# Moving the feed-forward's transposes from TensorE to 32 by 32 squares on VectorE and an exchange through DRAM

## The chip, the cores and the metric

The kernel runs on one core of a Trainium2 chip. The metric is the device time of one execution in microseconds (us); the time before is a median of three runs, 879.62 us (879.28 to 879.94). The engines are named as the profile names them: PE is TensorE (PEld its weight loads), DVE is VectorE, ACT is ScalarE, POOL is GpSimd, and SP issues the transfers ("SPq" is its queue). All are in-order; between engines an instruction waits for semaphores.

## The reference

Three layers work on x, 16 batches of 64 tokens with 512 features, each added to its input: cross-attention from a context of 512 tokens per batch, a differential self-attention, and a feed-forward whose operands are quantised to FP4 and back. Only the last concerns the change:

```python
def fp4_quant_dequant(x):                       # blocks of 16 along the last dim
    xb = x.reshape(shape[:-1] + (shape[-1] // BLOCK, BLOCK))
    scale = jnp.max(jnp.abs(xb), axis=-1, keepdims=True) / 6.0
    scale = jnp.maximum(scale, jnp.float32(1e-12))
    xn = xb / scale
    idx = jnp.searchsorted(_MID, jnp.abs(xn))
    q = _GRID[idx] * jnp.sign(xn) * scale

def fp4_linear(x, w):
    return jnp.einsum('bsk,nk->bsn', fp4_quant_dequant(x), fp4_quant_dequant(w))

x = x + fp4_linear(silu(fp4_linear(xn, w_gate)) * fp4_linear(xn, w_up), w_down)   # xn = layernorm(x)
```

The hidden width is 1408. Both activations, the normalised x and the hidden h, are quantised with the features along the free dimension, tokens on the partitions; the products want the features on the partitions. So both have to be transposed between the quantisation and the product that reads them.

## The kernel before

**Tiles and steps.** The 1024 tokens are eight tiles of 128. The hidden width is cut into three chunks of 512, 512 and 384 (`CHUNKS`). A step of the feed-forward is one (tile, chunk) pair; `FeedForward.steps` lists all 24: (0,0), (0,1), (1,0), (1,1), (0,2), (1,2), then (2,0), (2,1), (2,2) and so on to (7,2). The first three are spread by hand over the end of the self-attention, in `SelfAttention.rest`; `FeedForward.rest` calls `step(n)` for the others.

**One step.** Products run in three terms, high times high, high times low, low times high, over four 128-deep pieces: `terms`, L121, 12 matmuls for a chunk of 512. `gate` and `up` give 24 such matmuls into a PSUM pair. `gated` applies Silu on ACT (L1759) and the product with up on DVE (L1760). `quantise` calls `fp4_steps`: DVE's block maximum (L194), two small steps that make the scale and its shaded copy (L195, L196), the reciprocal (L197), the scaling by it (L199), a mask that keeps the exponent bits (L202), a Relu on ACT that turns them into a rounding constant (L205, called "the exponents' step" here), two scalar_tensor_tensor steps that round (L207, L208) and the scaling back (L210). All of h's DVE-capable steps are on DVE; for x both scalings are on POOL. `turn_h` for the step two back transposes h in 128 by 128 pieces on PE against an identity (L171) into PSUM, and `split` (L129, L130) makes the upper half by a rounding cast on ACT and the lower half by a subtraction on DVE. `down` for the step three back multiplies the halves with the down weights; after the third chunk the output tile is added up (L1812) and stored (L1813).

**x.** `norm(t+2)` is called in step (t,2): moments, the normalised tile, and the same quantisation with POOL's scalings. `turn(t+1)` transposes it on PE in step (t,1) and splits it.

**Order.** The scheduler orders each engine's instructions by a timing estimate of its own. At the end of `SelfAttention.rest`, `in_order` fixes the order of every engine's instructions as they are written up to there, by a dependence of each on the one before. What `FeedForward.rest` adds is free: the scheduler may put it between and in front of the fixed ones, and does. The last written lines of the fixed part are the upper half and product for (0,0)'s turn, the output product of tile 7 (`out(NT-1)`, the matmuls named wo) and the loads of the last weights; the loads of the third chunk's up-weights go into the slots that hold Wo until then.

**Buffers.** Gate and up alternate between two PSUM pairs. The halves of h have two buffers each (`two_h`, `two_l`). The exponents' tile `qe` is a single buffer (tag "one") that x and h share.

## Time and profile before

| | before |
|---|---|
| median of three runs | 879.62 us |
| the profiled execution's own time | 881.33 us |
| its span in the profile | 879.5 us |
| granted TensorE clock | 1.00 |
| matmuls for transposes of h (128x128) | 88, from 694.4 to 872.9 us |
| matmuls for transposes of x in the feed-forward | 32, from 665.7 to 836.1 us |
| output stores in the feed-forward, 256 KB each | 7, and 2 of 128 KB for the last tile |

The busy times on the page count the time in which an engine executes; matmuls are pipelined and their ends are modelled, so the start of one to the start of the next is the better measure of what an instruction costs PE. On the timeline a line is a group of like instructions: start, length, engine, line, operation, tiles, shapes, count, and in brackets the idle time before it and who ended it. The feed-forward's free part begins at about 694 us; from about 739 us on it repeats every 24.3 us, one token tile.

### The profile page before, as it was taken

To read this page: it belongs to the slowest core of one execution; us is meant where nothing else is said; L and a number is where in the kernel's file an instruction comes from. 1 tells how busy PE (TensorE), PEld (TensorE's weight loads), DVE (VectorE), ACT (ScalarE), POOL (GpSimd) and SP (SyncE) were. 2 spreads that over 40 slices of the span, in tenths; PEclk is the share of its full clock that TensorE was granted. 3 is DMA by queue.
4 is the path that set the end of the run, shared out by engine and by line. 5 is a ranking of instruction groups with operands and counts; after the bars stand their busy time and mean duration, and the time that the engine had idled before them with its cause. 6 is when DMAs were issued, how large, how long until landed. Compare 5 with 4: busy or idle time off the path is not lost.

```text
span 879.5 us, 17521 instructions
## 1 busy us (share of the span) xinstructions
PE 871.7 (99%) x6743; PEld 719.2 (82%) x6743; DVE 687.2 (78%) x1457; ACT 398.8 (45%) x787; POOL 296.2 (34%) x341
## 2 busy tenths in 40 slices
PE   8999999999999999999999999999999999999998
PEld 8988787878787888778878888888888888888887
DVE  7734457789788887787888867688998897888876
ACT  5654454544544535354445455554556233332221
POOL 2334234235353352353433622545543120111100
PEclk9999999999999999999999999999999999999999
DMA  8464554644655455435644362240008330000000
GB/s 277 167 233 169 167 163 142 201 143 141 192 164 160 138 174 168 136 111 178 183 134 149 121 198 64 82 192 1 1 3 320 136 144 13 13 13 13 13 12 25
DMA packets 80379, 111.12 MB, mean 126 GB/s; under 512 B 33176, under 2 KB 39080, under 8 KB 79016
## 3 DMA queue, kind: packets, MB, share of 16 engines
q1 hardware_dynamic: 80136, 109.48, 38.2%
q8 instruction: 53, 0.87, 0.4%
q0 software_dynamic: 160, 0.52, 0.2%
q14 instruction: 30, 0.25, 0.1%
HBM read 84.26 MB, written 25.72 MB: 125 GB/s over the span
## 4 chain that ended last, share of the span: by engine, by line
PE 93%; DVE 3%; DMA 2%; ACT 1%; POOL 1%; issue 1%; SPq 0%; ACTq 0%; DVEq 0%; POOLq 0%
PE pv L121 20%; PE pk L121 19%; PE gu L121 13%; PE dn L121 6%; PE sim L967 4%; PE av L1055 4%; PE Wv L121 3%; PE wo L121 3%; PE po L121 2%; PE Wq L121 2%; PE Wk L121 2%; PE prt L1004 2%; PE lq L121 2%; PE lk L121 2%; PE lv L121 1%; PE ht L171 1%
## 5 line engine op out<-in xcount | busy, mean ns | idle before, releaser
L121 PE MATMUL pv<-xvh,x 128*128 128x512 f32 x512 | 133.0, 394 | 0.0
L121 PE MATMUL pk<-x,xkh 128*128 128x512 f32 x512 | 128.2, 392 | 0.0
L121 PEld LDWEIGHTS pv<-xvh,x 128*128 128x128 f32 x512 | 94.8, 188 | 26.2 <-issue 7.0
L121 PEld LDWEIGHTS pk<-x,xkh 128*128 128x128 f32 x512 | 94.9, 188 | 19.5 <-issue 0.4
L990 ACT ACTIVATE pr<-pr,least 128x576 f32<-128x576 f32 x64 | 49.1, 769 | 59.7 <-DVE least L986 59.7
L941 DVE TENSOR_TENSOR k<-pk,row 128x512 f32<-128x512 f32 x64 | 43.2, 675 | 39.2 <-PE pk L121 39.0
L368 POOL TENSOR_TENSOR x<-raw,x 128x512 fp32r<-128x512 f32 x32 | 41.6, 1301 | 85.8 <-ACT x L362 80.5
L121 PE MATMUL pv<-xvl,x 128*128 128x512 f32 x256 | 68.7, 390 | 0.0
L121 PE MATMUL pk<-x,xkl 128*128 128x512 f32 x256 | 68.5, 389 | 0.0
L954 ACT ACTIVATE v<-pv,rs 128x512 f32<-128x512 f32 x64 | 43.2, 684 | 54.8 <-PE pv L121 54.3
L121 PE MATMUL gu<-uT,fx 128*128 128x512 f32 (+1 forms) x288 | 67.0, 377 | 0.2 <-DMA uT<-u_d 0.2
L121 PE MATMUL gu<-gT,fx 128*128 128x512 f32 (+1 forms) x288 | 65.8, 376 | 0.0
L121 PEld LDWEIGHTS gu<-gT,fx 128*128 128x128 f32 x288 | 52.2, 188 | 7.6 <-ACT fx L129 0.2
L121 PEld LDWEIGHTS gu<-uT,fx 128*128 128x128 f32 x288 | 51.8, 188 | 7.7 <-DMA uT<-u_d 0.5
L121 PEld LDWEIGHTS pv<-xvl,x 128*128 128x128 f32 x256 | 48.0, 188 | 10.3
L121 PEld LDWEIGHTS pk<-x,xkl 128*128 128x128 f32 x256 | 48.1, 188 | 10.2
L986 DVE CUSTOM_DVE_ANT_0 pr<-sim,mask 128x576 f32<-128x576 f32 x64 | 45.8, 753 | 5.3 <-PE sim L967 4.3
L205 ACT ACTIVATE qe_h<-qe_h,mmagic 128x512 f32<-128x512 f32 (+1 forms) x24 | 16.5, 687 | 66.7 <-DVE qe_h L202 64.6
L321 DVE BATCH_NORM_STATS2 cst<-nat 128x6 f32<-128x512 f32 x64 | 42.8, 669 | 3.7 <-DMA nat<-in_ctx_dram 3.7
L121 PE MATMUL dn<-dT,hh 128*128 128x512 f32 x170 | 42.9, 392 | 0.0
L967 PE MATMUL sim<-k,mask 64*64 64x288 f32 x512 | 40.4, 415 | 0.3 <-DMA mask<-q_d 0.3
L362 ACT CAST x<-raw 128x512 fp32r<-128x512 f32 x64 | 39.1, 631 | 0.0
(347 smaller groups left out, 1867.1 us busy)
## 6 DMA issues: line engine op xcount, KB each, us to landing
nat<-in_ctx_dram SPq DMA_DIRECT2D x16, 1024.0 KB
raw<-in_ctxT_dram SPq DMA_DIRECT2D x64, 256.0 KB
d_d<-qhl_d SPq DMA_DIRECT2D x11, 512.0 KB
row<-rs_d SPq DMA_DIRECT2D x16, 256.0 KB
g_d<-qhl_g SPq DMA_DIRECT2D x8, 512.0 KB
u_d<-qhl_u SPq DMA_DIRECT2D x8, 512.0 KB
gT<-g_d SPq DMA_DIRECT2D x4, 1024.0 KB
uT<-u_d SPq DMA_DIRECT2D x4, 1024.0 KB
```

The source lines that it names most:

```text
L121: self.nc.tensor.matmul(ps, lhsT=p[i], rhs=p[j], start=start and n == 0, stop=stop and n == last)
L205: nc.scalar.activation(e, e, AF.Relu, bias=self.mmagic, scale=MAGIC)
L321: nc.vector.bn_stats(st, self.nat[b][:, j, :])
L362: self.cm.nc.scalar.copy(self.done[b][0][:, c, :], self.raw[:, c, :])
L368: by.tensor_tensor(lo, self.raw[:, c, :], f32(hi), ALU.subtract)
L941: nc.vector.tensor_tensor(k[:, S : S + N], ps, cx.row[b], ALU.mult)
L954: nc.scalar.mul(v, ps, cx.rs[b][:, t : t + 1])
L967: nc.tensor.matmul(pss[r][c * S : (c + 1) * S, h, :half], lhsT=queries[b % 2][rows, m, :], rhs=st["k"][m][rows, at : at + half], start=Tru ...
L986: nc.vector.tensor_tensor_reduce(two(pr), ps[:, :, :half], two(mask), -1.0, BIG, ALU.add, ALU.min, least)
L990: nc.scalar.activation(pr, pr, AF.Exp, bias=least, scale=-1.0, accum_out=st["tot"][:, t : t + 1])
L1004: nc.tensor.transpose(pt[:, c, at : at + S], state[b]["pr", a][rows, r, first + j * P : first + (j + 1) * P], cm.ident[rows, rows],)
L1055: nc.tensor.matmul(st["av"][r][rows, a, :], lhsT=prT[:, j, rows], rhs=st["v"][j][:, at : at + S], start=False, stop=j == NJ - 1, skip_grou ...
```

## The change

The transposes of x for tiles 3 to 7 and of h for 19 of the 24 steps (`far_steps`, all but the first three and the last two) leave PE. DVE transposes each 32 by 32 square in place within its block (`squares`), SP stores the result to DRAM in four pieces of 32 partitions, and loads it back with squares exchanged, into a tile with features on the partitions. `halves` makes the upper half with a copy on ACT and the lower half with a subtraction on POOL, both from SBUF. The copy is ordered behind the last written exponents' step (`behind`). In a step with a far turn, `turn_h` is written behind the quantisation and the sending of the current step; in the two steps past the end it is written behind `down`. The last scaling of a far h moves to POOL. Two small steps of every quantisation become scalar_tensor_tensor with a constant tile as second tensor. At the end of `FeedForward.rest`, PE's order is fixed as written, from the first instruction on.

```diff
+        self.least = const.tile([P, D // BLK], F32, tag="least", name="least")
+        nc.gpsimd.memset(self.least, 1e-12)
+        self.none = const.tile([P, D // BLK], F32, tag="none", name="none")
+        nc.gpsimd.memset(self.none, 0.0)
...
-    def in_order(self):
+    def in_order(self, *only):
 
         last = {}
         for ins in self.nc.cur_bb.bb.instructions:
+            if only and ins.engine not in only:
+                continue
...
-        nc.vector.tensor_scalar(s, m, 1.0 / 6.0, 1e-12, ALU.mult, ALU.max)
-        nc.vector.tensor_scalar(m, s, 1.0 + SHADE, None, ALU.mult)
+        least, none = (t[:, :nb] for t in (self.least, self.none))
+        nc.vector.scalar_tensor_tensor(s, m, 1.0 / 6.0, least, ALU.mult, ALU.max)
+        nc.vector.scalar_tensor_tensor(m, s, 1.0 + SHADE, none, ALU.mult, ALU.max)
...
+        self.sq = [dram(f"sq_d{n}", [4, 32, 4, KC * 32]) for n in range(4)]
...
+        self.far, self.far_steps = 0, self.steps[3:-2]
...
+    def newest(self):
+        return self.nc.cur_bb.bb.instructions[-1]
+
+    def behind(self, ins):
+        self.tc.add_manual_dep(
+            ins,
+            self.exponents.name,
+            mybir.DependencyInfo(mybir.DependencyClass.NoSync, mybir.DependencyReason.DATA),
+            reason="behind",
+        )
+
+    def squares(self, src, nk, pool, tag, home, name):
+        nc = self.nc
+        t = self.w1.tile([P, 4, KC * 32], F32, tag=tag, name=f"sq_{name}")[:, :, : nk * 32]
+        nc.vector.transpose(
+            t.rearrange("p q (k l) -> p q k l", l=32),
+            src.rearrange("p (k q l) -> p k q l", q=4, l=32),
+        )
+        far = self.sc.sq[self.far % len(self.sc.sq)][:, :, :, : nk * 32]
+        self.far += 1
+        for n in range(4):
+            nc.sync.dma_start(far[:, :, n].rearrange("q f r -> f q r"), t[n * 32 : (n + 1) * 32])
+        raw = pool.tile([P, 4, KC * 32], F32, tag=home, name=f"sr_{name}")[:, :, : nk * 32]
+        nc.sync.dma_start(raw, far.rearrange("q f t r -> (q f) t r"))
+        return raw
+
+    def halves(self, hi, lo, raw):
+        src = raw.rearrange("p t (k l) -> p k t l", l=32)
+        hi, lo = (x.rearrange("p k (t l) -> p k t l", l=32) for x in (hi, lo))
+        self.nc.scalar.copy(hi, src)
+        self.behind(self.newest())
+        self.nc.gpsimd.tensor_tensor(lo, src, f32(hi), ALU.subtract)
+
+    def send(self, t):
+        self.st["zs", t] = self.squares(self.st.pop(("z", t)), KC, self.w2, "k1", "four0", f"x_{t}")
+
+    def send_h(self, n):
+        s = self.steps[n]
+        if s in self.far_steps:
+            pool, home = ((self.w1, "k2"), (self.w2, "sq"))[n % 2]
+            nk = CHUNKS[s[1]][1] // P
+            self.st["hs", s] = self.squares(self.st.pop(("h", s)), nk, pool, "k0", home, f"h_{s[0]}_{s[1]}")
+
+    def regroup(self, t):
+        both = self.w2.tile([P, 2, KC, P], F32R, tag=f"fx{t % 2}", name=f"fx_{t}")
+        self.halves(both[:, 0], both[:, 1], self.st.pop(("zs", t)))
+        self.st["x", t] = both[:, 0], both[:, 1]
...
     def quantise(self, s):
         t, c = s
-        self.cm.fp4(self.w2, self.st["h", s], CHUNKS[c][1], f"h_{t}_{c}", tag="one")
+        w = self.st["h", s]
+        steps = self.cm.fp4_steps(
+            self.w2, w, CHUNKS[c][1], f"h_{t}_{c}", False, s in self.far_steps, tag="one"
+        )
+        for n, _ in enumerate(steps):
+            if n == 2:
+                self.exponents = self.newest()
...
     def turn_h(self, s):
...
+        self.st["hT", s] = hh, hl
+        if s in self.far_steps:
+            self.halves(hh, hl, self.st.pop(("hs", s)))
+            return
         pt = cm.tr(f"ht_{t}_{c}")
         cm.transpose_chunks(pt, self.st.pop(("h", s)), nk)
...
     def step(self, n):
         s = self.steps[n] if n < len(self.steps) else None
         if s:
             self.gate(s)
-        if 0 <= n - 2 < len(self.steps):
+        near = s and self.steps[n - 2] not in self.far_steps
+        if near:
             self.turn_h(self.steps[n - 2])
         if s:
             self.up(s)
             self.hidden(s)
+            self.send_h(n)
+        if s and not near:
+            self.turn_h(self.steps[n - 2])
+        if s:
             if s[1] == 2 and 2 <= s[0] < NT - 2:
                 self.norm(s[0] + 2)
+                self.send(s[0] + 2)
             elif s in ((1, 1), (0, 2)):
                 self.norm(1 + s[1])
+                if s[1] == 2:
+                    self.send(1 + s[1])
         if 0 <= n - 3:
             self.down(self.steps[n - 3])
+        if not s and n - 2 < len(self.steps):
+            self.turn_h(self.steps[n - 2])
         if s and (s == (1, 2) or (s[1] == 1 and 2 <= s[0] < NT - 1)):
-            self.turn(s[0] + 1)
+            if s[0] == 1:
+                self.turn(s[0] + 1)
+            else:
+                self.regroup(s[0] + 1)
 
     def rest(self):
         for n in range(3, len(self.steps) + 3):
             self.step(n)
+        self.cm.in_order(mybir.EngineType.PE)
```

## The prediction

> **What bounds the kernel now.** I read the page's busy table first, then TensorE's timeline through the feed-forward, then ACT, DVE and POOL over the same stretches, then the busy time of each engine by stage.
>
> ```profile
> span 879.5 us, 17521 instructions
> PE 871.7 (99%) x6743; PEld 719.2 (82%) x6743; DVE 687.2 (78%) x1457; ACT 398.8 (45%) x787; POOL 296.2 (34%) x341
> 763.20:787.60 24.40, 24.40 (x124) 20.95 (x122) 21.57 (x47) 7.22 (x12) 2.21 (x2) 1.00 0.03 12
> ```
>
> TensorE bounds it. The third line is one token tile of the feed-forward (columns: window, length, then PE, PEld, DVE, ACT, POOL busy, clock, DMA share, GB/s): PE has no gap, DVE is busy 21.57 of 24.4 us, POOL 2.21. So work taken off PE counts in full, and every new wait of PE counts in full too. Only two PE gaps of any size stand after 694 us: 0.18 for the last up-weights and 0.41 at the very end.
>
> **What is removed.** By start-to-start times of the PE timeline four transposes take 0.36 us of the engine (694.51 to 694.87), three take 0.245 (854.37 to 854.62). Moved off are twelve 4-chunk and seven 3-chunk blocks of h, and x for tiles 3 to 7: 17 x 0.36 + 7 x 0.245 = 7.84 us. The 0.18 wait goes too (below): 8.0 us gained. The Trainium skill speaks against such a move: "VectorE: DVE Perf Modes", Rules for kernel authors, gives a 128x128 transpose to TensorE where PSUM will do, and its section on the three paths prices one on TensorE at 390 ns (bf16). By that figure 89 of them would save an estimated 34.7 us; the trace's 0.09 us apiece decides.
>
> **What TensorE's fixed order costs at the start.** Before, the scheduler slid the feed-forward's gate and up in front of the last output product; in the order written that product (wo of tile 7) comes straight after the ht transposes of chunk (0,0).
>
> ```profile
> 694.51 0.60 PE L171 MATMUL ht<-ident,h 128*128 128x128 f32 x4
> 694.87 2.98 PE L121 MATMUL gu<-gT,fx 128*128 128x512 f32 x12
> 697.68 2.88 PE L121 MATMUL gu<-uT,fx 128*128 128x512 f32 x12
> 700.40 1.07 PE L121 MATMUL wo<-Woh,oh 128*128 128x512 f32 x4
> ...
> 695.84 0.72 ACT L205 ACTIVATE qe_h<-qe_h,mmagic 128x512 f32<-128x512 f32 x1 [3.69 <-DVE qe_h L202]
> 696.46 0.76 ACT L1529 ACTIVATE oT<-ot,lnwb 128x512 f32<-128x512 f32 x1
> 697.26 0.62 ACT L1539 CAST oh<-oT 128x512 fp32r<-128x512 f32 x1
> ```
>
> wo needs oh, which ACT ends at 697.88, behind a relu that waits on DVE. ACT's order there is already fixed and is not touched. PE stands from 694.87 to about 698.0: 3.1 us. wo then ends at 700.7, not 703.6; the last up-weights reuse Wo's slots, so their load starts 2.9 us sooner and lands near 708.5, before it is wanted at 711: the 0.18 is gone. Next, turn(2) now stands right before gate (2,0). From the start of an xt to the first matmul that reads its cast is 1.37 us (723.41 to 724.78 in the trace, then covered by four down matmuls): 1.37 - 0.36 = 1.0 us open.
>
> **What the hold costs at the end.** The upper half of chunk (7,0) now stands on ACT behind the exponents of (7,2), whose chain starts when up (7,2) ends at 864.80. Before, that cast was done during up (7,2).
>
> ```profile
> 864.80 1.55 PE L121 MATMUL dn<-dT,hh 128*128 128x512 f32 x6
> ...
> 866.89 0.60 PE L171 MATMUL ht<-ident,h 128*128 128x128 f32 x4
> 867.24 2.10 PE L121 MATMUL dn<-dT,hh 128*128 128x512 f32 x8
> ...
> 870.10 1.98 PE L121 MATMUL dn<-dT,hh 128*128 128x512 f32 x8
> ```
>
> By DVE's rows the chain is: silu 0.2 to 0.69 after the end of up, product to 1.29, reduce to 1.87, two small steps and reciprocal 0.76, scaling 0.59, mask 0.39, hop 0.09, relu 0.62: 4.3. The cast adds 0.6, the hop 0.1: PE can go on at 5.0, while down (6,2) is over at 2.05: 2.9 us of hole. (With the output add queued inside the chain, as it was before, when relu ended at 870.80, it is 4.6.) Then turn_h of (7,1) stands directly before its own down: 1.0 us again. The last chunk's 0.41 stays. Holes: 3.1 + 1.0 + 2.9 + 1.0 = 8.0, all of the gain. **The one-off parts come to nothing:** 0, or +1.7 with the longer chain.
>
> **What happens in the tiles between.** Per tile PE's own work falls from 24.3 us to 23.0: three blocks of four transposes and one of three, 3 x 0.36 + 0.245 = 1.3. The down product of chunk n-3 waits for an upper half that is held behind the exponents of chunk n-1. That chain from the end of up is 5.06 us to the end of relu (857.45 to 862.51), plus 0.6 and 0.1: 5.8. PE has down + gate + up in that time: 2.73 + 2 x 2.19 = 7.1 at the shortest. So there is 1.3 us of slack, and if DVE is undisturbed the hold costs nothing. Behind the held cast ACT has the next chunk's silu, which PE wants only a step later. DVE's square waits for POOL's scaling, and behind it stands the next chunk's product with up, the head of the very chain: what POOL delays, PE's down product pays. But the change also moves work to POOL: per tile three last scalings of h (1.06, 1.06, 0.84 us by POOL's L199 and L210 rows), three lower halves (1.29, 1.29 and, by width, about 0.97, from POOL's two-tensor rows L1405 and L368) and one lower half of x (1.29): 7.8 us beside the 2.2 of now. And POOL and DVE block each other:
>
> ```profile
> 803.98 1.06 POOL L210 TENSOR_TENSOR fz<-fz,qs_x 128x512 f32<-128x512 f32 x1 [6.48 <-DVE qm_h L196]
> 804.35 1.24 DVE L199 TENSOR_TENSOR h<-h,qm_h 128x512 f32<-128x512 f32 x1
> ...
> 796.35 1.15 POOL L199 TENSOR_TENSOR fz<-fz,qm_x 128x512 f32<-128x512 f32 x1 [15.34 <-DVE qm_x L197]
> 796.62 1.09 DVE L202 TENSOR_SCALAR qe_h<-h 128x384 uint32<-128x384 uint32 x1
> ```
>
> A DVE scaling that takes 0.69 alone takes 1.24, ending 0.55 after POOL does; the mask (0.36 alone) takes 1.09. Both lie in the chain. DVE's transposes, reduces and operations from PSUM keep their times beside POOL in this trace (transpose 0.65 to 0.71 with or without). The Trainium skill, "SBUF — State Buffer", Who interferes with whom, says that a DVE instruction with two SBUF inputs or in a two-port mode and a GpSimd instruction that reads SBUF shut each other out for a whole instruction. The rows agree; by that rule alone each POOL instruction would be charged in full, an estimate of 20 us over five tiles.
>
> Now 2.2 us of POOL in a tile block DVE for 0.55 + 0.73 = 1.28, a ratio of 0.6; 7.8 more give 4.7. DVE's own work per tile: 21.2 (mean of three tiles) less 1.93 (scaling), 1.93 (lower halves) and 0.69 (x), plus transposes 3 x 0.70 + 0.57 (rows L287): 19.3. With the blocking 24.0. DVE also waits for relu, 13.7 us over the 24 chunks, 1.7 a tile; with half of it filled, DVE needs 24.8 a tile. Against PE's 23.0 that is 1.8 a tile. Bounds: 0 where every POOL instruction falls into DVE's free stretches; 19.3 + 7.8 = 27.1, so 4.1 a tile, where each blocks in full. I take the ratio that the trace shows: tiles 2 to 6, 5 x 1.8 = 9.
>
> **Costed at nothing.** Per chunk four 64 KB stores and one 256 KB load on SP's queue. SP has only seven output stores in this stretch; issues take 0.33 us, and the last stores, issued by 877.07, are over before 879.5, so at most 2.5 us each way: 5 x 0.33 + 5 = 6.7. The cover is from DVE's square (about 9.6 us after up n) to the exponents of n+2 (16 + 5): 11 us. Uncovered, 1 us late is 1 us on each of 19 chunks. A load waits on SP for its four stores and for the lower half of n-2, whose buffer it fills; an output store queued behind it delays nobody before the next tile's. The two small rewrites, 67 quantisations x 2 x 0.18 us: bounds 0 and, if each took 0.05 more, 7 us in all on a DVE that is seven to nine tenths busy in cross-attention under a full PE, hidden there. The added constants lie before the first matmul: nothing.
>
> **The sum:** the profiled execution took 881.33 (span 879.5); -8.0 + 8.0 + 9 gives 890.3. That execution is 1.7 above the median shown, so on the median 879.62 + 9 = 888.6.
>
> **Rivals.** (A) The lock falls into DVE's gaps and only the one-off parts count: 879.6 to 881.4. For it: 1.3 us of slack. Against: the scalings and masks that were hit with only two POOL instructions a tile. (B) Faster: the order written does not reach back to wo and turn(2), because the scheduler still fills those two holes; then 4.1 us of holes are gone, and with A's empty lock 875.5. It decides from PE's idle time before wo: under 1.5 us the change can gain. Against: the chain is drawn over every TensorE instruction of the block. (C) The exchange is late by more than its 11 us cover: at 13 us, 2 us x 19 = 38, near 918. Against: the 2.5 us. (D) Nearly every POOL instruction hits the chain, 4.1 us a tile, 20 in all: 897 to 902 with the longer chain at the end.
>
> **How the numbers follow.** Forecast (883 to 897) 0.55, D 0.15, A 0.15, B 0.10, C 0.05. A measurement of this kernel can tell 0.2%, 1.8 us, from no change. Faster: B, 0.10. Same, 877.9 to 881.4: most of A and a little beside, 0.10. Slower: 0.80. The range leaves out B and C and the upper edge of D: 879 to 904; the forecast's own is 883 to 897.
>
> **What would show it.** PE idle about 3 us before wo of tile 7, 1 before gate (2,0), 3 before the first down (7,0) matmul, 1 before down (7,1), each released by ACT's cast. In tiles 2 to 6, PE waits at dn for hh, tile periods near 24.8 instead of 23.0, DVE scalings and masks above 1 us beside POOL. Wrong if periods are 23.0 (A), if the gap before wo is missing (B), or if hh waits for a DMA (C).

## The result, and the profile after

The changed kernel takes 899.43 us (median of four, 898.98 to 900.08), the kernel before 879.60 beside it: a ratio of 1.0226, 95% interval 1.0208 to 1.0244. The forecast was 888.6 with a range of 879 to 904: the direction is right, the loss is 19.8 us where 9 were forecast.

The profiled execution after (900.08 us, span 898.3) stands against the one before (881.33, span 879.5): 18.8 us more span. The page of after, to be read against the page lines of before:

```profile
span 898.3 us, 17600 instructions
PE 870.7 (97%) x6654; PEld 714.5 (80%) x6654; DVE 701.9 (78%) x1438; ACT 397.0 (44%) x787; POOL 346.8 (39%) x386
```

TensorE has 89 matmuls less, as many as the transposes that were moved, and yet only 1.0 us less busy time: some of the remaining ones became longer. POOL has 50 us more. All of TensorE's waits after 690 us, in the timeline of after (start, length, engine, line, output and inputs, count, and in brackets the idle time in front and who ended it):

```profile
697.76 1.20 PE L127 MATMUL wo<-Woh,oh 128*128 128x512 f32 x4 [2.88 <-ACT oh L1547]
727.60 5.49 PE L127 MATMUL gu<-gT,fx 128*128 128x512 f32 x12 [3.37 <-ACT fx L135]
758.50 2.11 PE L127 MATMUL dn<-dT,hh 128*128 128x512 f32 x8 [0.41 <-ACT hh L1764]
768.90 2.11 PE L127 MATMUL dn<-dT,hh 128*128 128x512 f32 x8 [1.96 <-ACT hh L1764]
784.48 2.11 PE L127 MATMUL dn<-dT,hh 128*128 128x512 f32 x8 [0.86 <-ACT hh L1764]
794.89 3.58 PE L127 MATMUL dn<-dT,hh 128*128 128x512 f32 x8 [1.94 <-ACT hh L1764]
820.86 2.14 PE L127 MATMUL dn<-dT,hh 128*128 128x512 f32 x8 [1.52 <-ACT hh L1764]
836.45 2.14 PE L127 MATMUL dn<-dT,hh 128*128 128x512 f32 x8 [0.86 <-ACT hh L1764]
846.52 2.14 PE L127 MATMUL dn<-dT,hh 128*128 128x512 f32 x8 [1.58 <-ACT hh L1764]
883.05 3.10 PE L127 MATMUL dn<-dT,hh 128*128 128x512 f32 x8 [4.39 <-ACT hh L1764]
888.83 2.11 PE L127 MATMUL dn<-dT,hh 128*128 128x512 f32 x8 [0.73 <-ACT hh L135]
892.58 1.44 PE L1894 MATMUL dn_last<-dT,hh 128*128 128x256 f32 x9 [0.41 <-ACT hh L1850]
```

Three things are to be read here. The bracketed times sum to 20.9 us (before: 0.59): 6.25 at the start, 9.13 in the tiles between, 5.12 at the end, and the 0.41 that was there before. Every one of them is ended by an ACT cast: L1764 is the held upper half. And the lengths: twelve gate matmuls take 5.49 at 727.60, eight down matmuls 3.58 at 794.89 where their like take 2.11. By start-to-start times these and the matmuls behind them cost 6.3 us more than the same work elsewhere: gate and up (2,0) 5.28 + 3.17 for 2.72 + 2.73 (3.0 us), the down product at 794.89 3.39 for 1.82 (1.6), the one at 883.05 2.90 + 1.55 for 1.82 + 0.91 (1.7).

The sum of the profile: -7.84 (transposes) + 20.3 (idle) + 6.3 (slow matmuls) = 18.8, the whole difference of the spans.

The granted clock of the gate product (2,0) and of the gate product of the next tile, by windows (window, length, then PE, PEld, DVE, ACT, POOL busy, clock, DMA share, GB/s):

```profile
727.60:732.88 5.28, 5.28 (x12) 4.18 (x13) 5.09 (x9) 2.51 (x4) 2.07 (x2) 0.50 0.37 92
752.49:755.21 2.72, 2.72 (x14) 2.25 (x13) 2.70 (x9) 0.00 (x0) 1.69 (x2) 1.00 0.02 10
```

The gate behind the hole of 3.37 us ran at half clock for all of its 5.28 us, and the sum of the prediction has no term for that.

Which holes are followed by such a stretch, the record shows too. In each of the twenty traces kept for this case, the times at which the granted clock changes lie whole multiples of 3.41 us apart; in after it falls at 726.88, 795.15 and 883.89, and comes back at 733.71 (two multiples later), 798.56 and 887.31. So the time can be cut into windows on that grid. Here are, in the same columns, two windows of after that share the hole in front of wo, two at the hole before 794.89, and two of e4_before_order (below), where the hole in front of wo lies in one window:

```profile
692.75:696.16 3.41, 2.13 (x14) 1.64 (x12) 2.62 (x7) 0.49 (x1) 0.00 (x0) 1.00 0.00 0
696.16:699.58 3.42, 1.82 (x8) 1.51 (x9) 3.09 (x5) 2.02 (x4) 0.00 (x0) 1.00 0.00 0
791.73:795.15 3.42, 1.48 (x7) 0.94 (x6) 2.20 (x5) 2.24 (x4) 0.23 (x1) 1.00 0.25 65
795.15:798.56 3.41, 3.41 (x9) 2.64 (x9) 3.38 (x4) 0.18 (x1) 2.10 (x2) 0.50 0.42 105
```
```profile
694.56:697.97 3.41, 0.59 (x3) 0.48 (x3) 2.46 (x5) 2.50 (x4) 0.00 (x0) 1.00 0.00 0
697.97:701.38 3.41, 3.41 (x9) 2.65 (x8) 3.24 (x8) 0.00 (x0) 0.00 (x0) 0.50 0.00 0
```

The hole of 2.88 us leaves 1.28 and 1.60 us idle in its two windows, and the clock stays; the one of 1.94 lies in one window, and the next runs at 0.50. Over all the traces, a window at full clock with more than 1.87 us idle was followed by one at half clock every time (34 of 34), and one with less never (some 5000); of two at 1.87, one was (in e20_late_nohold) and one was not (in e3_both_dve). A slow window was followed by a second one where 0.72 us or more of it were idle, and by full clock where 0.54 or less were. A slow window full of work costs half of its 3.41 us, 1.7 us. The kernel after has four of them with 0.72 us idle in one, by estimate (4 x 3.41 - 0.72) / 2 = 6.5 us, against the 6.3 read off the matmuls.

The tiles 2 to 6 of after, gate (t,0) to gate (t+1,0), in the same columns:

```profile
727.60:752.49 24.89, 24.89 (x103) 21.02 (x104) 18.81 (x31) 6.89 (x12) 7.70 (x7) 0.88 0.32 85
752.49:778.03 25.54, 23.18 (x107) 19.20 (x106) 22.20 (x39) 6.81 (x12) 10.58 (x10) 1.00 0.30 86
778.03:805.58 27.55, 24.75 (x107) 20.36 (x105) 23.49 (x41) 6.91 (x12) 12.13 (x11) 0.94 0.30 83
805.58:829.99 24.41, 22.89 (x107) 19.29 (x106) 21.43 (x38) 6.24 (x11) 9.06 (x9) 1.00 0.32 91
829.99:855.66 25.67, 23.23 (x107) 19.21 (x105) 22.66 (x39) 6.13 (x11) 10.65 (x10) 1.00 0.31 88
```

A tile takes 25.6 us on average, not the 24.4 of before; the second and the fifth row show TensorE with 23.2 us of work in it, as was worked out (23.0), and 2.4 us idle.

**How a tile loses its 2 us.** DVE and POOL of after in the stretch ahead of the wait at 794.89 (DVE's rows, then POOL's):

```profile
784.55 1.66 DVE L215 SCALAR_TENSOR_TENSOR h<-h,qe_h 128x384 f32<-128x384 f32 x1
786.32 1.10 DVE L209 TENSOR_SCALAR qe_x<-fz 128x512 uint32<-128x512 uint32 x1
787.34 0.68 DVE L1821 TENSOR_TENSOR h<-gu,h 128x512 f32<-128x512 f32 x1
...
791.02 1.23 DVE L206 TENSOR_TENSOR h<-h,qm_h 128x512 f32<-128x512 f32 x1
```
```profile
784.51 1.29 POOL L1766 TENSOR_TENSOR hl<-sr_h,hh 128x512 fp32r<-128x512 f32 x1 [1.51 <-ACT hh L1764]
786.29 0.84 POOL L217 TENSOR_TENSOR h<-h,qs_h 128x384 f32<-128x384 f32 x1 [0.49 <-DVE h L215]
790.64 1.06 POOL L217 TENSOR_TENSOR fz<-fz,qs_x 128x512 f32<-128x512 f32 x1 [3.51 <-DVE qm_h L203]
```

The held cast releases POOL's lower half at 784.51, and DVE's square (L215, 0.55 us alone at this width) takes 1.66 beside it. The square's end releases POOL's last scaling at 786.29, and DVE's mask of x takes 1.10 beside that. Behind both stands the product with up (L1821), the head of the next chain, whose silu ACT had ended at 784.93: it starts at 787.34, 2.4 us after that; 1.1 us of this are what the square took too long, 0.7 what the mask did. The scaling by the reciprocal (L206) then meets POOL once more (1.23), this time x's last scaling, which was on POOL before the change. At the end of this chain stands the cast that TensorE waits 1.94 us for.

### The profile page after: what moved, and what is told of

Read it like the earlier page. It is cut to its first block, busy times and chain, and to the rows that moved or that the text cites. A ratio compares the mean times of both kernels' runs of the same rounds, so it can differ in the third digit from the quotient of the medians.

```text
span 898.3 us, 17600 instructions
## 1 busy us (share of the span) xinstructions
PE 870.7 (97%) x6654; PEld 714.5 (80%) x6654; DVE 701.9 (78%) x1438; ACT 397.0 (44%) x787; POOL 346.8 (39%) x386
## 4 chain that ended last, share of the span: by engine, by line
PE 68%; DVE 21%; ACT 4%; issue 3%; POOL 2%; DMA 2%; SPq 0%; DVEq 0%; ACTq 0%; POOLq 0%
PE pv L127 17%; PE pk L127 17%; PE sim L975 4%; PE av L1063 3%; DVE h L215 3%; PE Wv L127 2%; PE lv L127 2%; PE po L127 2%; PE Wq L127 2%; PE Wk L127 2%; PE lq L127 2%; PE lk L127 2%; PE prt L1012 2%; ACT qe_h L212 2%; PE wo L127 2%
## 5 line engine op out<-in xcount | busy, mean ns | idle before, releaser
L127 PE MATMUL gu<-uT,fx 128*128 128x512 f32 (+1 forms) x288 | 64.6, 373 | 0.0
L212 ACT ACTIVATE qe_h<-qe_h,mmagic 128x512 f32<-128x512 f32 (+1 forms) x24 | 16.5, 687 | 107.8 <-DVE qe_h L209 107.8
L127 PEld LDWEIGHTS gu<-gT,fx 128*128 128x128 f32 x288 | 54.5, 194 | 12.1 <-ACT fx L135 3.6
L127 PE MATMUL dn<-dT,hh 128*128 128x512 f32 x170 | 46.3, 415 | 14.3 <-ACT hh L1764 13.5
L127 PEld LDWEIGHTS dn<-dT,hh 128*128 128x128 f32 x170 | 32.3, 196 | 24.5 <-ACT hh L1764 17.2
L1766 POOL TENSOR_TENSOR hl<-sr_h,hh 128x512 fp32r<-128x512 f32 (+1 forms) x19 | 23.2, 1220 | 67.6 <-ACT hh L1764 54.2
```

Source lines behind the costliest of these rows:

```text
L127: self.nc.tensor.matmul(ps, lhsT=p[i], rhs=p[j], start=start and n == 0, stop=stop and n == last)
L212: nc.scalar.activation(e, e, AF.Relu, bias=self.mmagic, scale=MAGIC)
L1766: self.nc.gpsimd.tensor_tensor(lo, src, f32(hi), ALU.subtract)
```

## The experiments

Each kernel below is the one after with the edit shown, unless it is said otherwise; times are medians beside runs of the kernel before on the same chip (880.3 to 880.5 there). Holes are TensorE's idle times after 690 us. The kernel before differs by up to 0.9 us between the chips, so what is said below to "come back" is good to about 1 us.

| kernel | us | ratio to before (95%) |
|---|---|---|
| after | 899.43 | 1.0226 (1.0208 to 1.0244) |
| e1_free: TensorE's order not fixed | 892.75 | 1.0144 (1.0127 to 1.0161) |
| e2_nohold: no hold | 892.74 | 1.0141 (1.0126 to 1.0156) |
| e3_both_dve: lower halves and last scalings on DVE | 890.82 | 1.0116 (1.0101 to 1.0131) |
| e5_lo_dve: lower halves alone on DVE | 890.67 | 1.0118 (1.0102 to 1.0133) |
| e9_tail: nothing held at the end | 892.17 | 1.0128 (1.0111 to 1.0145) |
| e7_ts: small rewrites undone | 899.55 | 1.0220 (1.0205 to 1.0236) |
| e8_noxch: exchange left out | 900.19 | 1.0223 (1.0207 to 1.0238) |
| e10_fill, e16_fill15: the hole filled | 904.02, 899.45 | 1.0256 (1.0237 to 1.0276), 1.0205 (1.0188 to 1.0223) |
| e4_before_order: before, order fixed | 888.70 | 1.0093 (1.0078 to 1.0108) |
| e11_free_nohold_tail | 884.40 | 1.0043 (1.0028 to 1.0058) |
| e12_plus_lo_dve | 882.10 | 1.0016 (1.0006 to 1.0025) |
| e13_x_on_pe | 881.44 | 1.0001 (0.9987 to 1.0015) |
| e14_x_earlier | 880.53 | 0.9997 (0.9983 to 1.0012) |
| e15_x_only | 880.05 | 0.9990 (0.9979 to 1.0000) |
| e18_h01 | 881.38 | 1.0009 (1.0000 to 1.0019) |
| e19_late_order | 877.19 | 0.9962 (0.9948 to 0.9975) |
| e20_late_nohold | 881.15 | 1.0012 (1.0002 to 1.0022) |

**1. The order alone, and without it.** e4_before_order is the kernel before with only this added at the end of `rest`; e1_free is the kernel after with only this taken out:

```diff
+        self.cm.in_order(mybir.EngineType.PE)
```

> The kernel before with TensorE's order fixed as written, nothing else of the change. Theory A: holes of 2.9 before wo and 1 to 3.4 before gate (2,0), with up to 3 of slow clock, and 2 at the end, where the last transposes stand before a down product: 885 to 890. Rival B (the order alone is harmless, the holes need the held casts): 879 to 881.

> The changed kernel without the last fixing of TensorE's order; hold, exchange and POOL's share stay. Theory A (three causes add up: order 2.9 + 3.4 us of holes and 3.0 us of slow clock at the start, the hold with POOL's blocking in the tiles, the hold at the end): the start's 9 us come back, tile holes and the end stay, 889 to 892. Rival B (order is the main cause, since a free scheduler also fills the tile holes with gate and up products): 880 to 884. Rival C (order costs nothing, PE waits for the same things anyway): 898 to 901.

The order alone costs the kernel before 8.2 us. Its trace has the hole in front of wo at 2.82, and, which the prediction did not have, the wo product behind it slow (4.45 us for its twelve matmuls, 2.7 elsewhere); then 0.68 at gate (2,0) and 2.46 in front of the last transposes. Taken out of the kernel after, 6.7 us come back, less than the 9 that theory A adds up (892.75, just above its range): the hole in front of wo is gone and that of gate (2,0) falls to 1.11, but the holes in front of the down products stay and are longer (4.14, 2.37 and 2.54 are the longest; 10.4 us in the tiles for 9.1). So the order carries the start, and the tiles' loss has another cause.

**2. The hold.**

```diff
         self.nc.scalar.copy(hi, src)
-        self.behind(self.newest())
```

> The changed kernel without the hold of the upper halves behind the exponents' step. Theory A: PE waits for these casts only because of the hold, the exchanged data being there some 10 us earlier; tile holes (9.1 us, 1.7 of slow clock) and the hole at the end (4.4 and 1.7) go, the start's 9 us stay: 882 to 886. Rival B (the exchange itself is late, or the cast in front of silu on ACT's queue makes the chain late): no better than the changed kernel, 897 to 905.

6.7 us come back, where theory A expected 13 to 17. In the tiles only holes of 1.01, 0.71 and 1.21 are left, but at the end one of 4.46 stays, now for another reason: the exchange of (7,0) is on the path there (stores from 869.04, the load at 872.25, the cast at 874.85: 5.8 us from the first store to the cast). So near to the end nothing covers an exchange.

**3. POOL's new work.** e3_both_dve has both edits, e5_lo_dve the first alone:

```diff
-        self.nc.gpsimd.tensor_tensor(lo, src, f32(hi), ALU.subtract)
+        self.nc.vector.tensor_tensor(lo, src, f32(hi), ALU.subtract)
...
-            self.w2, w, CHUNKS[c][1], f"h_{t}_{c}", False, s in self.far_steps, tag="one"
+            self.w2, w, CHUNKS[c][1], f"h_{t}_{c}", False, False, tag="one"
```

> The changed kernel with the last scaling of h and all lower halves on DVE; POOL keeps only the two scalings of x, as before the change. Theory A (POOL's added instructions block DVE in the held chain): the second rounding step falls from 1.5 us back to 0.7, tile holes fall from 9.1 us to 2 to 5, the end's hole from 4.4 to 3: 891 to 895. Rival B (DVE's plain load is the limit: 22.6 us a tile of its own work and 1.3 blocked against PE's 23.0): tile periods above 26, 900 to 908.

> The kernel after, fixed order and hold kept, with only the lower halves moved from POOL back to DVE; POOL keeps the last scalings of h. (With both back on DVE it was 890.8.) Theory A (the lower halves do the damage, since they are released by the held cast, at the very moment when DVE is in the scalings of the next chain): 890 to 893, most of TensorE's waits of 0.8 to 2 us a tile gone, and the second step of the squaring back at 0.69 us from 1.5. Rival B (the last scalings on POOL block DVE as often): 894 to 898, with half of the waits left.

The two come out alike: the lower halves on POOL cost 8.8 us, and the last scalings cost as much on POOL as on DVE. That is a balance and not nothing. With the scalings on POOL the hole before gate (2,0) is 2.79 us (e5_lo_dve), on DVE it is 0.68 (e3_both_dve), for a reason shown further down; the holes in the tiles are 2.5 and 5.1 us. The group of DVE's square between 730 and 865 us, of after and then of e5_lo_dve (count, busy us, mean ns of one, idle time in front):

```profile
L215 DVE SCALAR_TENSOR_TENSOR h<-h,qe_h 128x512 f32<-128x512 f32 x10 | 15.0, 1497 | 0.3
```
```profile
L215 DVE SCALAR_TENSOR_TENSOR h<-h,qe_h 128x512 f32<-128x512 f32 x11 | 7.5, 684 | 0.0
```

1497 ns against 684. The seven tile holes with their 9.13 us shrink to four of 0.62, one a tile. One tile of e5_lo_dve and one of e3_both_dve, by windows:

```profile
751.46:775.29 23.83, 23.21 (x106) 19.23 (x105) 21.48 (x44) 6.91 (x12) 6.05 (x6) 1.00 0.34 95
```
```profile
748.46:772.91 24.45, 23.15 (x107) 19.20 (x105) 22.39 (x47) 6.81 (x12) 2.22 (x2) 1.00 0.34 91
```

With the last scalings on DVE too, DVE has more to do (22.4 us for 21.5) and the tile is longer by 0.6. The 0.62 that remains in e5_lo_dve is, by the rows, due to POOL's scaling of x, which was there before the change: it stands beside the mask of the third chunk (1.09 us from 779.15, beside POOL's 1.18 from 778.85), in a chain that TensorE did not wait for then. No run took that scaling off POOL, so this is not shown.

**4. The end.**

```diff
-        self.far, self.far_steps = 0, self.steps[3:-2]
+        self.far, self.far_steps = 0, self.steps[3:-3]
...
+        if n == len(self.steps):
+            self.turn_h(self.steps[n - 2])
         if 0 <= n - 3:
             self.down(self.steps[n - 3])
-        if not s and n - 2 < len(self.steps):
+        if n == len(self.steps) + 1:
             self.turn_h(self.steps[n - 2])
```

> The kernel after, with three chunks instead of two kept on TensorE at the end, so that no cast is held there, and the turn of chunk (7,1) before the down product of (7,0). Theory A (the hole of 4.4 us at the end and the slow matmuls after it, 1.7 us, belong to the held cast of (7,0)): 4 to 5 us come back less 0.36 of transposes, 894 to 896. Rival B (DVE's chain for the last chunks sets the end in any case, and the wait goes from the cast to the transposes of (7,1)): 2 us or less come back, 897 to 900.

7.3 us come back. Theory A's cause is right, its figure too small: at the end only the 0.41 is left, so 4.39 + 0.73 of idle and 1.7 of slow matmuls went, less 0.36 of transposes 6.5 us (6.3 by the two spans). Rival B fell.

**5. The small rewrites, and the exchange.** e7_ts writes the two small operations with `tensor_scalar` again. e8_noxch leaves the stores and the load out, so the halves come from the squares as DVE left them and the product is not that of the reference:

```diff
-        nc.vector.scalar_tensor_tensor(s, m, 1.0 / 6.0, least, ALU.mult, ALU.max)
-        nc.vector.scalar_tensor_tensor(m, s, 1.0 + SHADE, none, ALU.mult, ALU.max)
+        nc.vector.tensor_scalar(s, m, 1.0 / 6.0, 1e-12, ALU.mult, ALU.max)
+        nc.vector.tensor_scalar(m, s, 1.0 + SHADE, None, ALU.mult)
```

> The kernel after, with the two small rewrites taken back (the maxima are scaled by operations with one tensor operand again). The prediction costed them at nothing. Theory A (they stay at 0.18 us on DVE and lie beside TensorE): 898 to 901. Rival B (with two tensor operands they are blocked by POOL in the chain that TensorE waits for): 0.2 to 0.4 us a chunk come back, 892 to 896. A third way, C (with one tensor operand they are blocked more, as 0.42 us operations went to 1.5 in the kernel before): 901 to 904.

> The changed kernel without the stores to DRAM and the loads back: the halves are made from the squares as they lie, so the exchange between squares is left out of the computation. Theory A (the transfers are hidden, PE waits for held casts): 897 to 901. Rival B (the transfers or their queue are late and hold the casts up): 893 or less, and the waits for hh are shorter.

Neither can be told from after (+0.1 and +0.8 us, the intervals overlap). In the kernel after the exchange is hidden, and the rewrites are free.

**6. The slow matmuls.** Idle matmuls in front of gate (2,0), 40 in e10_fill and 14 in e16_fill15, their product read by nobody:

```diff
+        if t == 2:
+            fill = cm.tr("fill")[:, :P]
+            for _ in range(14):
+                cm.nc.tensor.matmul(fill, lhsT=cm.ident, rhs=cm.ident, start=True, stop=True)
```

> The changed kernel with 40 idle products of 128x128 against the identity on PE behind the transposes of x for tile 2, some 3.6 us in the 3.4 us hole before gate (2,0). Theory A (the low granted clock after a hole comes from PE having stood still): the 12 matmuls of gate (2,0) take 2.7 us again instead of 5.3, 896 to 898. Rival B (the clock falls for another reason there): 899 to 900.5.

> The kernel after with 14 idle matmuls (128 x 128, about 3 us) put into TensorE's hole of 3.4 us in front of gate (2,0), and nothing else changed. Their product is read by nobody. Theory A (the slowdown of gate and up (2,0), 5.28 + 3.17 us for 2.73 + 2.2, follows from the hole): the twelve gate matmuls take under 3.0 us, and the kernel 895 to 898. Rival B (the clock falls there for another reason, for instance by a window of its own): gate (2,0) still takes over 4 us, 899 to 901.

Forty took 8.85 us, far beyond the hole (the gate behind them took 2.86 us). Fourteen fit; the profile shows each as two records. TensorE's rows of e16_fill15, and the window of its gate product:

```profile
723.74 3.29 PE L1790 MATMUL fill<-ident 128*128 128x128 f32 x28
727.26 3.01 PE L127 MATMUL gu<-gT,fx 128*128 128x512 f32 x12 [0.23 <-ACT fx L135]
```
```profile
727.26:730.11 2.85, 2.85 (x12) 2.36 (x13) 2.81 (x6) 0.67 (x1) 1.15 (x1) 1.00 0.28 69
```

The gate starts at nearly the same time, 727.26 for 727.60, with the clock at 1.00 and 2.85 us for its twelve matmuls where it had 0.50 and 5.28. Only what TensorE did in the 3.3 us ahead differs, so at this place the hole is what took the clock away. (For up (2,0) at full clock the expectation says 2.2 us; it is 2.73.) As a time the fill is worth nothing certain: the profiled execution, the fastest of four, is 2.3 us of span shorter, but the median is that of after, 899.45, in rival B's range. Slow matmuls came after another hole instead (the down product at 766.79, 2.70 for 1.82 and 1.71 for 0.91), which in after had stayed fast: its 1.91 us lie in one window of the grid, where in after 1.96 us were split into 0.89 and 1.06 (768.90). The hole in front of wo, 2.82 to 2.89 us in every kernel with the order fixed from the start, goes the same way: it is followed by slow matmuls where 2.09 us or more of it lie in one window (e2_nohold, e4_before_order, e5_lo_dve, e7_ts, e8_noxch, e9_tail, e10_fill), and not where it is at most 1.87 (after, e3_both_dve, e16_fill15).

**7. What is left when the causes go.** e11_free_nohold_tail has no order, no hold and the end of e9_tail; e12_plus_lo_dve also the lower halves on DVE; e13_x_on_pe also x's transposes on TensorE again; e14_x_earlier, instead, x's normalising and stores one step earlier:

```diff
-            if s[1] == 2 and 2 <= s[0] < NT - 2:
+            if s[1] == 1 and 2 <= s[0] < NT - 2:
```

> The changed kernel without the fixed order, without the hold, with (7,0) transposed on PE again and the turn of (7,1) in front of the down of (7,0). POOL keeps its share. Theory A (order, hold and end are the costs, POOL's blocking reaches PE only through the hold): tile periods 23.0 to 23.5, 873 to 879. Rival B (the blocking makes DVE late enough by itself): periods of 24 and more, 880 to 888.

> As the run before, with the lower halves on DVE; the last scaling of h stays on POOL. Theory A (the second rounding step is blocked by POOL's lower halves, 0.8 to 1.0 us a chunk, about what a lower half costs DVE, 0.69): the same as the run before within 2 us. Rival B (DVE's load decides): 3 or more slower; rival C (blocking decides): 3 or more faster.

> The kernel after without the fixed order, without the hold, with the lower halves on DVE and three chunks' exchange left off at the end (the best version so far, 882.1), and now all transposes of x back on TensorE; only h is exchanged. Theory A (what was left there, 5 to 6 us of holes, was x's exchange landing 1 to 1.5 us late in each tile): those holes go, x's transposes put 4 x 0.36 + ... = about 5 x 0.36 = 1.8 us back on TensorE, so 877 to 880, and TensorE's idle time before gate (t,0) falls under 0.4 us a tile. Rival B (DVE, at 22 to 23 busy of 24 us a tile, is the bound, and moving x off its transposes only shifts the wait): 881 to 884, with waits at the down products for the cast of the upper half.

> The same best version so far (882.1), x still exchanged, but its normalising and its stores one chunk earlier in each tile. Theory A (x's load lands late and only that): the 1 to 1.5 us of hole in front of each gate (t,0) go, 876 to 879. Rival B (DVE has no room at the earlier place, so h's chain is pushed back instead): the holes move to the down products, 881 to 885.

e11_free_nohold_tail falls into rival B (periods of 23.2, 24.6 and 24.7 us); the 2.3 us of e12_plus_lo_dve lie between its theories A and C. The first two have holes of 0.29 to 1.53 at gate (t,0), because x's load lands late: in e12_plus_lo_dve the stores of one x start at 809.41, its cast waits 4.19 us for the load and starts at 815.16, the gate at 815.83. With x on TensorE, or sent earlier, those holes go, as theory A said of both, but the medians (881.44 and 880.53) stay at the kernel before. In e14_x_earlier holes of 1.09, 0.56, 0.73 and 0.25 stand at the down products instead, as its rival B said. The profile of e13_x_on_pe is the fastest of its ten executions (878.48; they spread to 883.56), so its holes, 2.74 of 5.2 us in front of the transposes of (7,1), don't explain its median. The mean clock on record does in part: it is 0.999 and 1.000 for the two fastest, 0.996 to 0.998 for the other eight, and one slow window is 0.002 of it and 1.7 us. The rest stays open.

**8. Less moved.** e15_x_only exchanges x alone (h's list of far steps is empty), with the edits of e12_plus_lo_dve in the tiles, x sent earlier and the rewrites undone. e18_h01 exchanges only the chunks 0 and 1 of h:

```diff
-        self.far, self.far_steps = 0, self.steps[3:-2]
+        self.far, self.far_steps = 0, [s for s in self.steps[3:-3] if s[1] != 2]
```

> Only x of tiles 3 to 7 goes by DVE's squares and the exchange, h stays on TensorE as in the kernel before; no fixed order, no hold, lower halves on DVE, the two small rewrites taken back. It takes 5 x 0.36 = 1.8 us off TensorE and nothing else. Theory A (one exchange a tile, sent a chunk earlier, is fully hidden): 877.5 to 879. Rival B (its load still lands late, or DVE's squares push h's chain into TensorE): 880 to 884.

> A version meant to beat both: no fixed order, no hold, lower halves on DVE, x on TensorE, and only the chunks 0 and 1 of h (512 wide) through the exchange; the 384 wide chunk, whose transposes cost TensorE 0.245 us and DVE 0.57, stays on TensorE. Theory A (DVE is the bound of the version with all chunks, at 22 of 23 us a tile, and is relieved by some 0.6 us a tile): 877 to 879.5. Rival B (the waits only move): 880 to 883, with holes of more than 2 us at the end as before.

Neither can be told from the kernel before, or only just: the first takes at most 1.8 us of transposes away, of which 0.4 arrives (880.05, at the edge of rival B); and e18_h01, meant to relieve DVE, keeps 1.91 us at the end and 1.3 at gate (2,0). Theory A fell in both.

**9. Order and hold kept where they serve.** e19_late_order is the kernel after with the lower halves on DVE, the end of e9_tail, and the order fixed only from chunk (2,1) on; e20_late_nohold is the same without the hold:

```diff
-    def in_order(self, *only):
+    def in_order(self, *only, start=0):
...
-        for ins in self.nc.cur_bb.bb.instructions:
+        for ins in list(self.nc.cur_bb.bb.instructions)[start:]:
...
+            if self.steps[n : n + 1] == [(2, 1)]:
+                start = len(self.nc.cur_bb.bb.instructions)
             self.step(n)
-        self.cm.in_order(mybir.EngineType.PE)
+        self.cm.in_order(mybir.EngineType.PE, start=start)
```

> The kernel after with what the other runs point to: lower halves on DVE, three chunks kept on TensorE at the end with the turn of (7,1) before the down product of (7,0), and TensorE's order fixed only from chunk (2,1) on, so that the scheduler is free at the start. Order and hold are kept in the tiles between, x and h are exchanged. Theory A (the parts add up: from 890.7 with the lower halves on DVE, 7 come back at the end as they did alone, and 5 to 7 at the start, the hole of 2.9 before the last output product and most of the one of 2.8 before gate (2,0), with the slow matmuls after both): 876 to 879, below the kernel before. Rival B (one bound takes over, DVE at 22 to 23 us a tile, and the waits come back in the tiles): 881 to 884.

> The same without the hold: ACT may make an upper half as soon as its scheduler thinks the load is there. Theory A (with the lower halves on DVE the hold costs the 0.6 us a tile that were seen, and no more): 1 to 3 us below the version with the hold. Rival B (without it ACT's casts stand in front of the exponents and wait there for their loads, as they did for 2 to 4 us in the version without order and hold): the same or up to 4 us above, with holes at gates or transposes.

877.19 us, ratio 0.9962 (0.9948 to 0.9975): 3.1 us faster than before on this chip, and the one version that is faster beyond its interval. Its page, and its tile 4 by windows:

```profile
span 875.1 us, 17587 instructions
PE 864.2 (99%) x6658; PEld 710.5 (81%) x6658; DVE 691.4 (79%) x1462; ACT 396.9 (45%) x787; POOL 316.6 (36%) x361
```
```profile
767.87:791.73 23.86, 23.21 (x107) 19.24 (x105) 21.27 (x43) 6.92 (x12) 5.58 (x6) 1.00 0.34 94
```

Four holes of 0.62 or 0.63, 1.20 at gate (2,0), 0.3, 0.28 and the 0.41: 4.7 us in all, and no slow matmul. By the sum, -7.84 + 0.36 (one chunk more on TensorE) + 4.1 = -3.4; the medians have -3.1 (the spans -4.4, but the profiled execution of before lay 1.7 above its median). So the parts add up, and no new bound takes over (rival B).

Without the hold 4 us are lost again. ACT, in e20_late_nohold, runs its casts in the order that the scheduler thought right, and waits there:

```profile
767.27 0.62 ACT L1764 CAST fx<-sr_x 128x512 fp32r<-128x512 f32 x1 [3.94 <-DMA sr_x<-sq_d]
767.80 0.72 ACT L212 ACTIVATE qe_h<-qe_h,mmagic 128x512 f32<-128x512 f32 x1
768.42 0.47 ACT L1819 ACTIVATE h<-gu 128x384 f32<-128x384 f32 x1
771.49 0.62 ACT L1764 CAST hh<-sr_h 128x512 fp32r<-128x512 f32 x1 [2.60 <-DMA sr_h<-sq_d]
```

A cast that waits 3.94 us for its load keeps the relu (L212) and the silu of the next chain behind it. With the hold these come first, and the load has landed when the cast's turn comes. TensorE's holes are 8.1 us without the hold for 4.7 with it: the new ones are 0.65, 1.87 and 1.03 in front of gates, each for x's cast, and 2.21 in front of the transposes of (7,1); the one of 1.87 is followed by a slow window. The hold, which costs 6.7 us in the kernel after, saves 4 where the lower half behind it is not on POOL. No run has this hold and DVE's lower halves without TensorE's fixed order in the tiles, so what that order is worth there stays open.

## Why the prediction was right, and where it failed

**Right: the transposes.** 89 matmuls went, and with their 7.84 us the sum of the profile closes; and the wait for the last up-weights did go.

**Right: the hole before wo**, 2.88 for 3.1, by the same cast. e4_before_order shows it without anything else of the change.

**Right in total, wrong in its division: the tiles.** The forecast took 1.8 us a tile, 9 in all; the holes sum to 9.13, and the period without the slow matmuls is 24.7 (25.6 less 4.6 us over five tiles) for a forecast of 24.8. But it spread all of POOL's 7.8 new us over DVE at a ratio of 0.6, and that the totals agree is luck. The runs show that of the 9.13 us 6.6 go with the lower halves (e5_lo_dve), while the last scalings cost no more on POOL than on DVE (e3_both_dve): the held cast and DVE's two rounding steps wait for the same relu, so the lower half, released by the cast, meets the square every time (17 of 17 between 730 and 870 us). That is no ratio but a fixed meeting, 0.7 to 1.1 us each.

**Mis-sized: "1.37 - 0.36 = 1.0 us open" before gate (2,0).** It was 3.37. The forecast counted the cast as free to start when the transposes end. What stood in front of it is a matter of ACT's queue. First after, ACT's rows and then DVE's:

```profile
726.35 0.72 ACT L212 ACTIVATE qe_x<-qe_x,mmagic 128x512 f32<-128x512 f32 x1 [2.51 <-DVE qs_h L202]
726.98 0.57 ACT L135 CAST fx<-xt 128x512 fp32r<-128x512 f32 x1
```
```profile
720.45 1.17 DVE L206 TENSOR_TENSOR h<-h,qm_h 128x384 f32<-128x384 f32 x1
721.65 1.10 DVE L209 TENSOR_SCALAR qe_h<-h 128x384 uint32<-128x384 uint32 x1
...
725.37 0.88 DVE L209 TENSOR_SCALAR qe_x<-fz 128x512 uint32<-128x512 uint32 x1
```

Then e3_both_dve, the same rows:

```profile
724.96 0.59 ACT L135 CAST fx<-xt 128x512 fp32r<-128x512 f32 x1 [0.89 <-PE xt L177]
726.61 0.72 ACT L212 ACTIVATE qe_x<-qe_x,mmagic 128x512 f32<-128x512 f32 x1 [0.35 <-DVE qm_h L203]
```
```profile
721.04 1.18 DVE L206 TENSOR_TENSOR h<-h,qm_h 128x384 f32<-128x384 f32 x1
722.25 1.10 DVE L209 TENSOR_SCALAR qe_h<-h 128x384 uint32<-128x384 uint32 x1
```

In after, the relu of a later tile's x stands ahead of the cast on ACT and waits for a mask that DVE ends at 726.25. In e3_both_dve DVE's scaling and mask are as slow, beside POOL's scalings of x, but the cast stands ahead of that relu and runs as soon as the transposes are done. ACT's order is not fixed in this part, the scheduler chose it. It goes with the hole in every kernel with TensorE's order fixed there and nothing put into the hole: relu first, 2.73 to 3.37 us (after, e2_nohold, e5_lo_dve, e7_ts, e8_noxch, e9_tail); cast first, 0.68 (e3_both_dve, e4_before_order). So what the forecast missed is ACT's queue. POOL's blocking lengthens the wait: against 0.56, 0.36 and 0.42 us for such rows where POOL is still, the three rows of after are 1.8 us too long, an estimate of what it adds. But it reaches TensorE only through that order. This is read off the rows: no run changed ACT's order alone.

**Mis-sized: the end**, "2.9 us of hole". It was 4.39, near the 4.6 that the forecast kept as its longer end: the output add did stand in the chain (DVE's L1882 at 879.48), and the square before it took 1.38 beside POOL. "1.0 us again" for (7,1) was 0.73.

**The step that failed: "The one-off parts come to nothing."** They were set at 8.0 us of holes against 8.0 of gain. The holes were 11.4, and TensorE's slow matmuls after the holes, for which the sum had no term, took 6.3 more (3.0 at gate and up (2,0), 1.6 in the tiles after it, 1.7 at the end). Of the 9.8 us between forecast and result by the spans (18.8 less 9), 6.3 are the clock, 2.15 the start, 1.2 the end, 0.1 the tiles. The granted clock was read before as a constant 1.00, as the page showed it; but a kernel without holes can't show what a hole does to it. The Trainium skill states it: "TensorE: Matmul & The Clock Gate", Part 1, has TensorE's clock halved after about 3.4 us of an idle window and given back after as long of work, with windows that run free. The clock of 0.50 after the hole of 3.37, and the grid of 3.41 us that lies differently from trace to trace, agree. That the window has to be idle does not: 1.9 us idle in a window with 1.5 us of work were enough (794.89 in after), and the measurement decides.

**Costed at nothing, rightly:** the exchange (e8_noxch) and the rewrites (e7_ts). But the exchange is hidden only while ACT's casts come late enough, which the hold sees to: without it the loads are waited for (e2_nohold at the end, e12_plus_lo_dve and e20_late_nohold in the tiles).

**The rivals.** A (no blocking) fell with the 9.13 us, B with the hole before wo, C with e8_noxch. D's time, 897 to 902, is what came, but for another reason: not every POOL instruction hits the chain; the holes in the tiles were of the forecast's size, and the clock (6.3 us) and longer holes at the start and the end (3.4) made the rest.

## What to carry to other kernels

A hole in TensorE's stream can be charged twice: its length, and 1.7 us of slow matmuls for each slow window behind it (here up to two). By these traces that came where more than 1.87 us of one window of 3.41 us were idle. So a hole shorter than that is charged once, one longer than twice 1.87 = 3.7 us (an estimate from it) twice wherever the grid lies, and one between them sometimes: it belongs into the range. Here an offload to POOL was priced by who runs on DVE at the moment it is released, not by its share of the time: the one released by the same event as the critical chain met it every time. And an order written by hand pays where it keeps a queue from waiting for a transfer, and costs where the scheduler had filled a wait with other work: leave it out there (e19_late_order).

## What the runs showed that was not expected

- The granted clock of TensorE changes on a grid of 3.41 us. Of two holes of like length in after, the one of 1.94 us, within one window, was followed by 0.50, the one of 1.96, split over two, was not; and 28 short matmul records in the hole of 3.37 us (3.29 us of them) kept the clock at 1.00.
- The last scalings of h gave the same time on DVE and on POOL (890.82 and 890.67), with DVE at 22.4 and 21.5 us of work in a tile; and the fastest version, e19_late_order, has DVE at 21.3 (21.57 in the tile shown of before).
- One execution can hide what a kernel does: ten executions of e13_x_on_pe lay 5 us apart (878.48 to 883.56), against 0.34 us for the five of e19_late_order (876.91 to 877.25), whose profile has no slow window.
